# A cross-attention loop in another order: the last scores chunk, the context products and the running maxima

## The chip, the cores and the metric

The kernel runs on one core of a Trainium2 chip. A core has five engines with their own in-order instruction streams: TensorE (PE, with its weight loads listed apart as PEld), VectorE (DVE), ScalarE (ACT), GpSimd (POOL) and SyncE (SP), which issues the DMAs here. The metric is the device time of one execution in microseconds, as the median over repeated runs.

## The reference

The program is a two-layer perceiver step on 16 batches of 64 latent tokens (width 512) and 16 contexts of 1601 tokens (width 256). The change lies in the first of its six stages, the first cross attention with its output projection:

```python
def _L0_xattn_ref(q, k, v, Wq, bq, Wk, bk, Wv, bv, Wo, bo):
    HEADS = 16                       # D_MODEL = 512, D_K = 32
    qh = (q @ Wq + bq).reshape(B, LQ, HEADS, D_K).transpose(0, 2, 1, 3)
    kh = (k @ Wk + bk).reshape(B, LKV, HEADS, D_K).transpose(0, 2, 1, 3)
    vh = (v @ Wv + bv).reshape(B, LKV, HEADS, D_K).transpose(0, 2, 1, 3)
    scores = jnp.einsum('bhqd,bhkd->bhqk', qh, kh) * scale
    attn = jax.nn.softmax(scores, axis=-1)
    out = jnp.einsum('bhqk,bhkd->bhqd', attn, vh)
    concat = out.transpose(0, 2, 1, 3).reshape(B, LQ, D_MODEL)
    return concat @ Wo + bo

x = x + _L0_xattn_ref(_layernorm(x, axis=-1), ctx_512, ctx_512, ...)
```

Behind it come a state-space block, a top-k feed-forward, a second cross attention, a causal self attention and a quantized gated feed-forward. None of their code is touched.

## The kernel before

The first attention is a loop over 32 units `u` (and a 33rd pass that only finishes the last one). A unit is one batch and one half of the heads: eight heads, whose 8 x 64 = 512 query columns form the free dimension. Keys lie on the partitions, in 13 chunks (`KC`): twelve of 128 keys and a last one of 65. The loop is a software pipeline of two units: unit `u` gets its keys, values, scores and running maxima, while unit `u - 1` gets its softmax and its context.

What one pass issues:

- **K**: `k_proj` (L205), eight blocks of two matmuls, each drained by ACT (L215) out of a bank of `ps_mm`. Between the first of them stand `maxima(u - 1)` (L275: four transposes into the bank of `ps_mx`, then a DVE reduction, L281) and `shift(u - 1)` (L283: four more transposes, then seven DVE additions, L294).
- **V**: `v_proj` (L217), 13 chunks of two matmuls, each drained by a DVE addition of the bias (L226) out of a bank of `ps_mm`. `ps_mm` has two banks in rotation, for K, V and the output projection alike, so a block waits until the block two before it was drained.
- **Scores**: `scores(u, g)` (L235), groups of four chunks in the four banks of `ps_sc`, one buffer; the 13th chunk is a group of its own (`g` = 3). Two ACT copies (L252) bring a group to `st`, an SBUF tile of 13 x 512 per partition.
- **Running maxima**: `running_max(u, k)` (L263), DVE: L268 takes the chunks 0 to 3, L270 two more chunks at a time (128 x 1024), L273 the last one (65 x 512), and L486 folds the two halves together.
- **Exponentials and their sum**: `exps(u - 1, k)` (L297): ACT in place (L302), and POOL adds the chunks into `acc` (L307, four times L309, L311, L312).
- **Context**: `attend(u - 1, 0)` and `attend(u - 1, 1)` (L314), 52 small matmul calls each, and `sum_up` (L326), which multiplies `acc` by ones and so needs POOL's L312. `divide` (L333, DVE) ends the unit.
- **Beside it**: one 128 x 512 piece of a later stage's weights is quantized per pass: `piece_scale` (DVE L164 to L166, POOL L167), `piece_round` in the next pass (DVE L171, POOL L172), with a load and a store on SP's queue. `diagonal` (POOL L260, four copies) spreads the queries of the next unit. `load_ctx` (L187, SP) brings the context of the batch after next.

Passes 5, 9, 13 to 29 also hold an output projection `project` (L340: eight matmul instructions in the trace, drained by DVE L345), passes 18 to 21, 30 and 31 a layer norm and its transposes, and the first eight passes an addition on POOL (L423).

The order is written out by hand in the loop (L403 to L488): `pin` keeps each engine's instructions in the order of the text, and every engine works its own list from top to bottom. [...] two banks `ps_mm`, four `ps_sc`, one `ps_av`, one `ps_mx`.

Of the kernel before, what the change touches and what calls it, by code (L numbers as in the profile page):

```python
# [9 lines left out]
F32 = mybir.dt.float32  # L10
AF = mybir.ActivationFunctionType
ALU = mybir.AluOpType
# [3 lines left out]
P = 128  # L16
# [4 lines left out]
KC = (LK + P - 1) // P  # L21
# [21 lines left out]
def nkeys(c):  # L43
    return min(P, LK - c * P)
# [3 lines left out]
def perceiver_kernel(ctx: ExitStack, tc: tile.TileContext, x_d, ctxT_d, ctx_d, cols_d, rows_d,  # L48
# [3 lines left out]
    v, s, pe, gp = nc.vector, nc.scalar, nc.tensor, nc.gpsimd  # L52

    def pool(stack, name, bufs=1, side="left", **kw):
        return stack.enter_context(
            tc.tile_pool(name=name, bufs=bufs, side=side, reuse_waits="tile", **kw))
# [50 lines left out]
    st = const.tile([P, G, 6], F32, name="st", tag="st")  # L107
# [54 lines left out]
    def piece_scale(n, pin=free):  # L162
        w, sc, inv = raw[n]
        pin(v.tensor_reduce(sc, w, AX.X, ALU.max, apply_absolute_value=True))  # L164
        pin(v.tensor_scalar(sc, sc, 1.0 / 7.0, 1e-12, ALU.mult, ALU.max))
        pin(v.reciprocal(inv, sc))  # L166
        pin(gp.tensor_tensor(w, w, inv.unsqueeze(2).to_broadcast([P, 16, 32]), ALU.mult))  # L167
# [10 lines left out]
    with ExitStack() as st1:  # L178
# [18 lines left out]
        ps_mm = pool(st1, "ps_mm", bufs=2, space=PSUM)  # L197
        pin = tc.keep_in_program_order

        def pmm(out, lhsT, rhs, start=True, stop=True):  # L200
            pin(pe.matmul(out, lhsT=lhsT, rhs=rhs, start=start, stop=stop))  # L201

        kts, vts, sts, rms, nms, accs, avs = {}, {}, {}, {}, {}, {}, {}
# [24 lines left out]
        def flat(u):  # L228
            return sts[u]

        def by_head(t):

            return t.rearrange("p (r i j q) -> p r j i q", r=2, i=2, j=2)

        def scores(u, g):  # L235

            ks = range(4 * g, min(4 * g + 4, KC))
            m = nkeys(ks[-1])  # L240
            if g == 0:
                sts[u] = stp.tile([P, KC, 512], F32, name="st", tag="st")
            st = sts[u]
            sc = ps_sc.tile([P, 2, 4, 2 * P], F32, name="sc", tag="sc")
            for k in ks:
                for i in range(2):
                    for r in range(2):
                        rows_ = slice(64 * r, 64 * r + 64)
                        pmm(sc[:m, r, k - ks[0], i * P:(i + 1) * P],
                            kts[u, i][rows_, k * P:k * P + m], qds[u % 2][rows_, i, :])  # L250
            for r in range(2):
                pin(s.copy(st[:m, ks[0]:ks[-1] + 1, r * 256:(r + 1) * 256], sc[:m, r, 0:len(ks)]))  # L252

        def diagonal(u):

# [7 lines left out]
        def running_max(u, k):  # L263

            f = flat(u)
            if k == 2:
                rms[u] = mxp.tile([P, 2, 512], F32, name="rm", tag="rm")
                pin(v.tensor_tensor(rms[u], f[:, 0:2, :], f[:, 2:4, :], ALU.max))  # L268
            elif k + 1 < KC:
                pin(v.tensor_tensor(rms[u], rms[u], f[:, k:k + 2, :], ALU.max))  # L270
            else:
                m = nkeys(k)
                pin(v.tensor_tensor(rms[u][:m, 0], rms[u][:m, 0], f[:m, k, :], ALU.max))  # L273
# [23 lines left out]
        def exps(u, k):  # L297

            n = min(2, KC - k)
            m = nkeys(k + n - 1)  # L300
            f = flat(u)
            pin(s.activation(f[:m, k:k + n, :], f[:m, k:k + n, :], AF.Exp))  # L302
            if u == 2 * B - 1:
                return
            if k == 2:
                accs[u] = mxp.tile([P, 2, 512], F32, name="acc", tag="acc")
                pin(gp.tensor_tensor(accs[u], f[:, 0:2, :], f[:, 2:4, :], ALU.add))  # L307
            elif 2 < k and n == 2:
                pin(gp.tensor_tensor(accs[u], accs[u], f[:, k:k + 2, :], ALU.add))  # L309
            elif n == 1:  # L310
                pin(gp.tensor_tensor(accs[u][:, 0], accs[u][:, 0], accs[u][:, 1], ALU.add))  # L311
                pin(gp.tensor_tensor(accs[u][:m, 0], accs[u][:m, 0], f[:m, k, :], ALU.add))  # L312

        def attend(u, i):  # L314

            st = sts[u]
            if i == 0:
                avs[u] = ps_av.tile([P, 2, 2, LQ], F32, name="av", tag="av")
            for k in range(KC):
                n = nkeys(k)  # L320
                for j in range(4):
                    e = (4 * i + j) * 32
                    pmm(avs[u][32 * j:32 * j + 32, 0, i, :], vts[u, k][:n, e:e + 32],
                        by_head(st[:n, k, :])[:, j // 2, j % 2, i, :], k == 0, k == KC - 1)

        def sum_up(u, parts):  # L326

            for z, (t, n) in enumerate(parts):
                for j in range(4):
                    pmm(avs[u][32 * j:32 * j + 32, 1, :, :], ones[:n, 0:32],  # L330
                        by_head(t[:n, :])[:, j // 2, j % 2, :, :], z == 0, z == len(parts) - 1)
# [54 lines left out]
        for m in range(4):  # L386
            for r in range(2):
                j = 2 * (m % 2) + r
                nc.sync.dma_start(
                    out=wo0[32 * j:32 * j + 32, m // 2::2, :],  # L390
# [5 lines left out]
        qds = [mxp.tile([P, 2, P], F32, name="qd", tag=f"qd{i}") for i in range(2)]  # L396
# [4 lines left out]
        ps_mx = pool(st1, "ps_mx", space=PSUM)  # L401

        for u in range(U + 1):  # L403
            old, new = u >= 1, u < U
            k_at = iter(range(0, KC, 2))

            def next_exps(n):
                for _ in range(n if old else 0):
                    exps(u - 1, next(k_at))

            def next_k(i, z):
                if old and new:
                    k_proj(u, i, z)

            def next_v(*ks):
                for k in ks:
                    if old or k >= EARLY:
                        v_proj(u, k)

            if new:  # L420
                diagonal(u)
            if u < G:
                pin(gp.tensor_tensor(x[:, u, :], x[:, u, :], row(R_BO0), ALU.add))  # L423

            normed = [(g, ln_norm(g, pin)) for g in NORM0.get(u, ())]
            next_k(0, 0)
            if old:
                maxima(u - 1)
            next_k(0, 1)
            if old:  # L430
                shift(u - 1)
            next_k(0, 2)
            for g, xn in normed:
                ln_transpose(g, xn, ps_mm, pin)
            next_k(0, 3)
            for z in range(4):
                next_k(1, z)
                next_exps((1, 1, 0, 2)[z])
            if not new:

                next_exps(3)
                attend(u - 1, 0)
                attend(u - 1, 1)
                sum_up(u - 1, [(flat(u - 1)[:, k, :], nkeys(k)) for k in range(KC)])
                divide(u - 1)
                break
            if old and u <= NPREP:
                piece_round(u - 1, pin)
            if u < NPREP:
                piece_load(u, prep)  # L450
            next_v(0, 1)
            scores(u, 0)
            next_exps(2)
            next_v(2, 3)
            running_max(u, 2)
            next_v(4, 5)
            if u >= 2 and (u - 2) % 4 == 3:
                g = (u - 2) // 4
                project(g)
                ln_stats(g, pin)  # L460
                if g in (3, 6):
                    ln_scale(0 if g == 3 else 4, g + 1, pin)
            scores(u, 1)
            next_exps(1)
            next_v(6, 7)
            running_max(u, 4)
            next_v(8)
            running_max(u, 6)
            next_v(9)
            if u < NPREP:  # L470
                piece_scale(u, pin)
            if old:
                attend(u - 1, 0)
            scores(u, 2)
            next_v(10, 11)
            running_max(u, 8)
            next_v(12)
            running_max(u, 10)
            scores(u, 3)
            if u % 2 and u // 2 + 2 < B:  # L480
                load_ctx(u // 2 + 2)
            if old:
                attend(u - 1, 1)
                sum_up(u - 1, [(accs[u - 1][:, 0], P)])
            running_max(u, 12)
            pin(v.tensor_tensor(rms[u][:, 0], rms[u][:, 0], rms[u][:, 1], ALU.max))  # L486
            if old:
                divide(u - 1)  # L488
        project(G - 1)
# [172 lines left out]
    with ExitStack() as st3:  # L662
# [78 lines left out]
        for q in range(2):  # L741
# [29 lines left out]
            for k in range(4):  # L771
                g = 4 * q + k
# [16 lines left out]
    with ExitStack() as st4:  # L789
# [81 lines left out]
        ps_mm = pool(st4, "ps_mm4", bufs=3, space=PSUM)  # L871
# [89 lines left out]
    mx = const.tile([P, 5, 24], F32, name="mx", tag="mx")  # L961
# [125 lines left out]
    with ExitStack() as st6:  # L1087
# [121 lines left out]
        last = psc.tile([P, D], F32, name="po", tag="pm")  # L1209
# [90 lines left out]
```

## Time and profile before

| what | us |
|---|---|
| median of 3 runs | 2069.85 (2067.97 to 2070.45) |
| the profiled execution | 2068.01 |
| its span, first to last instruction | 2066.3 |
| passes 1 to 31 of the loop, 75.70 to 1174.20 in the trace | 1098.5 |
| PE busy in that stretch | 1083.0 |
| DVE / POOL / ACT busy in that stretch | 801.9 / 717.7 / 543.9 |
| a pass with nothing extra (890.07 to 924.19) | 34.12 |
| a pass with a projection (924.19 to 962.58) | 38.39 |
| a pass with a layer norm (676.86 to 711.99) | 35.13 |

The granted TensorE clock is 0.987 over the span and 1.00 within the loop. Times in the trace count from the first instruction. A timeline line gives the start, the length, the engine, the source line and the names of the tiles; a number in brackets is the idle time of the engine ahead of it and what ended it. Lengths include a wait inside the instruction, so the same instruction can have two lengths; PE's ends are modelled, so blocks of matmuls are compared by their starts. In the trace one pass repeats the last to within some hundredths of a microsecond.

### The profile page before, as it was taken

The numbers are of one execution on the slowest core, as the hardware profiler recorded it, in microseconds if no ns is written. First come the engines' busy times: TensorE is split into PE (matmuls) and PEld (weight loads), VectorE is DVE, ScalarE is ACT, GpSimd is POOL, SyncE is SP. The second block draws the span as 40 slices with busy tenths as digits, with TensorE's granted clock in tenths as the row PEclk, the third lists the DMA queues.
The fourth block names the chain that finished last, engine by engine and source line by source line (L and its number), as shares of the span: only waits on it lengthen the run. The fifth ranks groups of instructions, "written<-read, shape, count | busy, mean of one in ns | idle before, by whom it ended". The sixth has DMA issues, their size and how long they took to land. (4 is left out here: it accounts for less than half of the span.)

```text
span 2066.3 us, 38999 instructions
## 1 busy us (share of the span) xinstructions
PE 1970.2 (95%) x17197; PEld 1230.0 (60%) x17197; DVE 1192.8 (58%) x1710; ACT 805.3 (39%) x1112; POOL 793.9 (38%) x494
## 2 busy tenths in 40 slices
PE   8899999999999999999999898899998999999779
PEld 4677677677777676776777654444454455444334
DVE  2587777677776767786776744712113334429751
ACT  2445354545455454545454543211101123317700
POOL 0377667576667575675766421300003000000100
PEclk9999999999999999999999899999999999999889
DMA  5011101110110111011100120510227971200001
GB/s 207 27 49 53 44 12 54 43 36 30 54 44 22 44 53 44 16 50 43 46 20 17 33 103 22 186 61 21 94 98 272 339 292 62 72 0 11 20 0 41
DMA packets 61755, 141.13 MB, mean 68 GB/s; under 512 B 4449, under 2 KB 31601, under 8 KB 60433
## 3 DMA queue, kind: packets, MB, share of 16 engines
q1 hardware_dynamic: 61584, 138.63, 19.0%
q8 instruction: 135, 2.21, 0.5%
q14 instruction: 36, 0.29, 0.0%
HBM read 127.02 MB, written 11.60 MB: 67 GB/s over the span
## 5 line engine op out<-in xcount | busy, mean ns | idle before, releaser
L201 PE MATMUL ps<-wkv,ctxT 128*128 128x256 f32 (+1 forms) x1664 | 396.5, 387 | 2.0
L201 PE MATMUL ps<-ctxT,wkv 128*128 128x400 f32 (+1 forms) x1024 | 368.2, 506 | 10.9 <-DMA ctxT<-in_ctxT_dram 8.6
L252 ACT COPY st<-sc 128x1024 f32<-128x1024 f32 (+1 forms) x256 | 205.6, 854 | 353.7 <-PE sc L201 353.6
L201 PEld LDWEIGHTS ps<-wkv,ctxT 128*128 128x128 f32 (+1 forms) x1664 | 296.5, 185 | 76.3 <-ACT kt L215 13.8
L226 DVE TENSOR_TENSOR vt<-ps,rows 128x256 f32<-128x256 f32 (+1 forms) x416 | 170.3, 416 | 244.9 <-PE ps L201 244.8
L309 POOL TENSOR_TENSOR acc<-acc,st 128x1024 f32<-128x1024 f32 x124 | 292.4, 2358 | 8.3 <-ACT st L302 1.5
L201 PEld LDWEIGHTS ps<-ctxT,wkv 128*128 128x128 f32 x1024 | 187.4, 191 | 141.6 <-issue 12.7
L294 DVE TENSOR_TENSOR st<-st,nb 128x1024 f32<-128x1024 f32 (+1 forms) x224 | 238.9, 1138 | 24.7 <-PE nb L288 24.7
L215 ACT ACTIVATE kt<-ps,cols 128x400 f32<-128x400 f32 (+1 forms) x256 | 152.4, 595 | 243.0 <-PE ps L201 243.0
L270 DVE TENSOR_TENSOR rm<-rm,st 128x1024 f32<-128x1024 f32 x128 | 224.7, 1755 | 0.0
L201 PE MATMUL sc<-qd,kt 64*128 64x128 f32 (+1 forms) x3328 | 218.3, 279 | 2.1 <-ACT st L252 2.1
L302 ACT ACTIVATE st<-st 128x1024 f32<-128x1024 f32 (+1 forms) x224 | 216.0, 994 | 7.1 <-DVE st L294 6.7
L201 PEld LDWEIGHTS sc<-qd,kt 64*128 64x128 f32 (+1 forms) x3328 | 192.2, 183 | 41.6 <-issue 34.2
L307 POOL TENSOR_TENSOR acc<-st 128x1024 f32<-128x1024 f32 x31 | 84.5, 2727 | 302.4 <-ACT st L302 168.1
L260 POOL COPY qd<-xnT 32x128 f32<-32x128 f32 x128 | 107.0, 836 | 38.8 <-DVE xnT L380 33.8
L201 PE MATMUL av<-st,vt 128*32 128x64 f32 x6656 | 110.0, 223 | 4.8 <-ACT st L302 4.8
L59 PE MATMUL ps<-xnT,w 128*128 128x512 f32 x256 | 112.2, 594 | 0.0
L201 PEld LDWEIGHTS av<-st,vt 128*32 128x32 f32 x6656 | 98.4, 112 | 22.1 <-issue 15.6
L59 PE MATMUL ps<-w,hT 128*128 128x512 f32 x256 | 110.2, 592 | 0.0
L1184 POOL TENSOR_TENSOR gate<-up,gate 128x1024 f32<-128x1024 f32 x4 | 9.5, 2384 | 258.6 <-ACT up L1183 258.6
L859 POOL TENSOR_TENSOR xw<-x,wb 128x512 f32<-128x512 f32 x8 | 9.9, 1268 | 210.3 <-ACT wb L852 210.3
L59 PE MATMUL po<-wdT,gate 128*128 128x512 f32 x192 | 85.4, 608 | 3.2 <-DVE gate L1206 3.2
(233 smaller groups left out, 2278.8 us busy)
## 6 DMA issues: line engine op xcount, KB each, us to landing
cT<-in_ctxT_dram SPq DMA_DIRECT2D x16, 1601.0 KB, 10.0
cN<-in_ctx_dram SPq DMA_DIRECT2D x16, 1536.0 KB, 9.6
ctxT<-in_ctxT_dram SPq DMA_DIRECT2D x15, 1601.0 KB, 7.8
grid<-w SPq DMA_DIRECT2D x36, 256.0 KB, 2.0
w<-grid SPq DMA_DIRECT2D x36, 256.0 KB, 2.6
w<-in_w_dram SPq DMA_DIRECT2D x2, 4096.0 KB
mk<-kept SPq DMA_DIRECT2D x16, 512.0 KB, 3.8
w<-in_wgate_dram SPq DMA_DIRECT2D x12, 256.0 KB, 2.6
```

The source lines that it names most:

```text
L59: pe.matmul(out, lhsT=lhsT, rhs=rhs, start=start, stop=stop)
L201: pin(pe.matmul(out, lhsT=lhsT, rhs=rhs, start=start, stop=stop))
L215: pin(s.activation(kts[u, i][:, o:o + n], ps[:, :n], AF.Identity, bias=col(C_BK0 + c)))
L226: pin(v.tensor_tensor(t[:n, :], ps[:n, :], row(R_BV0 + e, 256)[:n, :], ALU.add))
L252: pin(s.copy(st[:m, ks[0]:ks[-1] + 1, r * 256:(r + 1) * 256], sc[:m, r, 0:len(ks)]))
L260: pin(gp.tensor_copy(qds[u % 2][r, :, (j % 2) * LQ:(j % 2 + 1) * LQ], qo[r, c:c + 2, b * LQ:(b + 1) * LQ]))
L270: pin(v.tensor_tensor(rms[u], rms[u], f[:, k:k + 2, :], ALU.max))
L294: pin(v.tensor_tensor(f[:m, k:k + n, :], f[:m, k:k + n, :], nb[:m].unsqueeze(1).to_broadcast([m, n, 512]), ALU.add))
L302: pin(s.activation(f[:m, k:k + n, :], f[:m, k:k + n, :], AF.Exp))
L307: pin(gp.tensor_tensor(accs[u], f[:, 0:2, :], f[:, 2:4, :], ALU.add))
L309: pin(gp.tensor_tensor(accs[u], accs[u], f[:, k:k + 2, :], ALU.add))
L859: gp.tensor_tensor(xw, x[:, g, :], wb, ALU.mult)
```

## The change

`scores(u, 2)` now also computes the 13th chunk. Its two results go to two extra PSUM tiles, one in the bank of `ps_mx` and one in a bank of `ps_mm`, which so joins the rotation as one more block; two more ACT copies follow the two of the group. `scores(u, 3)` is gone. In the loop:

- V's chunks 4 and 5 come ahead of `running_max(u, 2)`; chunks 8 and 9 come ahead of `running_max(u, 4)` and `(u, 6)`.
- `scores(u, 2)` stands ahead of the context, and `attend(u - 1, 0)`, `attend(u - 1, 1)` and `sum_up` follow it in one run.
- The maxima of the chunks 8 to 11 come ahead of V's chunks 10 and 11, and V's chunk 12 comes behind the last maxima (L273 and L486).
- `load_ctx` is issued behind V's chunk 12.

The number of matmuls, copies, additions and DMAs is the same.

```diff
-            ks = range(4 * g, min(4 * g + 4, KC))
-            m = nkeys(ks[-1])
+            ks = range(4 * g, 4 * g + 4)
+            last = KC - 1
...
-            for k in ks:
+
+            def one_chunk(out, k):
+                n = nkeys(k)
                 for i in range(2):
                     for r in range(2):
                         rows_ = slice(64 * r, 64 * r + 64)
-                        pmm(sc[:m, r, k - ks[0], i * P:(i + 1) * P],
-                            kts[u, i][rows_, k * P:k * P + m], qds[u % 2][rows_, i, :])
+                        pmm(out[r][:n, i * P:(i + 1) * P],
+                            kts[u, i][rows_, k * P:k * P + n], qds[u % 2][rows_, i, :])
+
+            for k in ks:
+                one_chunk([sc[:, r, k - ks[0], :] for r in range(2)], k)
+            if last == ks[-1] + 1:
+                tail = [ps_mx.tile([P, 2 * P], F32, name="scl", tag="mx"),
+                        ps_mm.tile([P, 2 * P], F32, name="scl", tag="mm")]
+                one_chunk(tail, last)
             for r in range(2):
-                pin(s.copy(st[:m, ks[0]:ks[-1] + 1, r * 256:(r + 1) * 256], sc[:m, r, 0:len(ks)]))
+                pin(s.copy(st[:, ks[0]:ks[-1] + 1, r * 256:(r + 1) * 256], sc[:, r]))
+            if last == ks[-1] + 1:
+                n = nkeys(last)
+                for r in range(2):
+                    pin(s.copy(st[:n, last, r * 256:(r + 1) * 256], tail[r][:n]))
...
-            next_v(2, 3)
+            next_v(2, 3, 4, 5)
             running_max(u, 2)
-            next_v(4, 5)
...
-            next_v(6, 7)
+            next_v(6, 7, 8, 9)
             running_max(u, 4)
-            next_v(8)
             running_max(u, 6)
-            next_v(9)
             if u < NPREP:
                 piece_scale(u, pin)
+            scores(u, 2)
             if old:
                 attend(u - 1, 0)
-            scores(u, 2)
+                attend(u - 1, 1)
+                sum_up(u - 1, [(accs[u - 1][:, 0], P)])
+            running_max(u, 8)
+            running_max(u, 10)
             next_v(10, 11)
-            running_max(u, 8)
+            running_max(u, 12)
+            pin(v.tensor_tensor(rms[u][:, 0], rms[u][:, 0], rms[u][:, 1], ALU.max))
             next_v(12)
-            running_max(u, 10)
-            scores(u, 3)
             if u % 2 and u // 2 + 2 < B:
                 load_ctx(u // 2 + 2)
-            if old:
-                attend(u - 1, 1)
-                sum_up(u - 1, [(accs[u - 1][:, 0], P)])
-            running_max(u, 12)
-            pin(v.tensor_tensor(rms[u][:, 0], rms[u][:, 0], rms[u][:, 1], ALU.max))
             if old:
                 divide(u - 1)
```

## The prediction

> **What bounds the kernel now.** First the page: its span and TensorE's share.
>
> ```profile
> span 2066.3 us, 38999 instructions
> PE 1970.2 (95%) x17197; PEld 1230.0 (60%) x17197; DVE 1192.8 (58%) x1710; ACT 805.3 (39%) x1112; POOL 793.9 (38%) x494
> ```
>
> Then the busy times by stretch (stretch, its length, PE, PEld, DVE, ACT, POOL, clock, DMA): a plain pass of the loop, one with a projection, one with a layer norm.
>
> ```profile
> 890.07:924.19 34.12, 34.01 (x416) 24.95 (x412) 26.07 (x34) 17.17 (x23) 23.59 (x14) 1.00 0.16 60
> 924.19:962.58 38.39, 37.50 (x424) 26.46 (x421) 25.66 (x38) 17.17 (x23) 21.11 (x16) 1.00 0.08 20
> 676.86:711.99 35.13, 34.64 (x420) 25.39 (x416) 25.47 (x35) 17.65 (x24) 22.90 (x12) 1.00 0.15 58
> ```
>
> TensorE sets the pass. Only what opens or closes a gap in its stream can move the time; DVE (26 of 34 us) and POOL (24) matter where TensorE waits for them. The gaps are read from the timeline, engine by engine, over the end of one plain pass (its K began at 856.07):
>
> ```profile
> 880.99 1.66 PE L201 MATMUL av<-st,vt 128*32 128x64 f32 x104
> ...
> 884.56 3.18 PE L201 MATMUL ps<-wkv,ctxT 128*128 128x256 f32 x12
> ...
> 890.07 1.61 PE L201 MATMUL ps<-ctxT,wkv 128*128 128x401 f32 x4
> ...
> 886.67 0.62 PEld L201 LDWEIGHTS ps<-wkv,ctxT 128*65 128x65 f32 x4 [0.51 <-DVE vt L226]
> ...
> 879.71 2.96 DVE L270 TENSOR_TENSOR rm<-rm,st 128x1024 f32<-128x1024 f32 x1
> ...
> 882.92 1.95 DVE L270 TENSOR_TENSOR rm<-rm,st 128x1024 f32<-128x1024 f32 x1
> ...
> 886.93 1.61 DVE L270 TENSOR_TENSOR rm<-rm,st 128x1024 f32<-128x1024 f32 x1
> ...
> 888.80 1.21 DVE L270 TENSOR_TENSOR rm<-rm,st 128x1024 f32<-128x1024 f32 x1
> ...
> 876.79 4.80 POOL L309 TENSOR_TENSOR acc<-acc,st 128x1024 f32<-128x1024 f32 x2
> ...
> 881.66 2.13 POOL L311 TENSOR_TENSOR acc<-acc 128x512 f32<-128x512 f32 x1
> 883.87 2.14 POOL L312 TENSOR_TENSOR acc<-acc,st 65x512 f32<-65x512 f32 x1
> 886.41 1.05 POOL L167 TENSOR_TENSOR w<-w,winv 128x512 f32<-128x512 f32 x1 [0.40 <-DVE winv L166]
> ```
>
> TensorE loses 0.3 us here at V's chunk 12, which waits for a bias addition (12 V matmuls take 3.18 us, 2.86 in the projection pass). The four equal maxima take 2.96, 1.95, 1.61 and 1.21: the last is alone, the others wait in line with POOL. The first ends (882.67) 1.08 after the last L309 (881.59), the second (884.87) 1.08 after L311 (883.79), the third (888.54) 1.08 after L167 (887.46); L311 and L312, alone 1.3 or less, end 1.1 after the maximum before them. [...]
>
> **The rule and the rows.** [...] a waiting POOL gets in between two dependent maxima. Pass 0 shows it:
>
> ```profile
> 77.50 0.69 DVE L273 TENSOR_TENSOR rm<-rm,st 65x512 f32<-65x512 f32 x1
> 77.64 1.68 POOL L423 TENSOR_TENSOR x<-x,rows 128x512 f32<-128x512 f32 x1
> 78.23 1.64 DVE L486 TENSOR_TENSOR rm<-rm 128x512 f32<-128x512 f32 x1
> ```
>
> L486 comes 0.04 after L273, is 0.69 long alone, and takes 1.64: POOL slipped in. I take turns throughout. Costs from these rows: maximum 1.08 behind POOL, 1.22 alone; L311 1.12 and L312 1.14 behind DVE; L167 1.05, or 0.90 behind DVE (L172, of its shape, ends 0.90 after a maximum).
>
> **The change, plain pass, TensorE.** From the first context block (880.99) to the next K (890.07) is 9.08 now. New order, no waits: group 2 with chunk 12, 1.99 + 4 pairs at 0.11 = 2.43; context twice, 1.48 each (888.26 to 889.74); sum 0.33; V10 to V12 2.79: total 8.51. Fewer switches between blocks of different shape make the 0.57. The K block ahead of the transposes then lacks its first 0.1 and a 0.05 wait, the transposes 0.05: -0.21. Without a wait, -0.78 a pass.
>
> **DVE and POOL decide whether there is one.** V9's addition ends at 881.51 (0.11 after its block, plus 0.42) and the first maximum comes up at 881.44, while L309 holds the way. Its end moves from 881.59 to 881.66: the L268 maximum, now behind V5's addition, comes at 875.81, level with L309, and delays it; I let DVE win, as L171 at 867.33 did against L307 of 867.14 (2.82 for 2.36). Then in turn: maximum to 882.74, L311 to 883.86, maximum to 884.94, L312 to 886.08. L165 is held to L312's end (885.84 with 0.21 did so now), L166 ends at 886.41. The maximum of chunks 8, 9 starts at 886.33, ahead of L167 (886.48): ends 887.55. L167 to 888.45, the maximum of 10, 11 to 889.53. Only then V10's addition, to 889.87. With the extra score tile in the rotation, V12 has V10's bank, so it starts at 889.93, not at the 888.56 of the unhindered order: **a new wait of 1.37**. V12 takes 0.93, and K starts at 890.86, 0.79 later than now; less 0.21, **+0.58 a pass**.
>
> Hidden: the sum's wait for L312 (886.08 against 886.37; late by up to 1.3, it would only use up V12's wait). ACT copies of group 2 end at 885.0, before the maxima want them, of chunk 12 at 885.6, before V11 wants that bank at 887.6. The transposes wait for L486, 891.54, and come up at 892.2; the second K block wants V12's addition, 891.9, at 892.7; the shift wants L281, 893.7, at 894.0: cover of 0.3 to 0.8, the next to be late. POOL's instructions keep their order, with no DMA among them. The context load goes out about 1 us later in the pass, nothing but the next pass's piece stands behind it on SP, its data is wanted two passes on, and it takes 7.8 us: 0.
>
> **Projection pass.** Now the projection waits for V5's addition, which stands behind L268:
>
> ```profile
> 944.55 0.70 PE L201 MATMUL ps<-wo,xnT 128*128 128x512 f32 x1 [0.89 <-DVE vt L226]
> ...
> 952.54 1.22 DVE L270 TENSOR_TENSOR rm<-rm,st 128x1024 f32<-128x1024 f32 x1
> ```
>
> The V block ahead of it takes 4.61 (939.94 to 944.55), against 3.65 without the wait: **-0.96**, since the addition comes first. POOL has L311 and L312 behind it before V9 is done (the maximum of 952.54 has its 1.22), so DVE is not held: L166 ends at 956.87 on the new clock of this pass, both maxima and L167 at 960.15, V10's addition at 960.49, V12 starts at 960.55 where 960.44 would be free. K at about 961.4 instead of 962.58; beyond the 0.96 that is -0.2, and -0.1 at the transposes: **-1.25**. Pass 21 loses only 0.6 at that wait now: -0.85.
>
> **Layer-norm pass.** Nothing waits at V12 now (2.79), and the turns fall as in the plain pass: V block to 703.24, V10's addition to 712.15, V12 1.4 late, K at 713.1 instead of 711.99; less 0.15: **+1.0**.
>
> **Sum.** 19 plain passes (1 to 4, 6 to 8, 10 to 12, 14 to 16, 22 to 24, 26 to 28) at +0.58: +11.0. Passes 18, 19, 20, 30 at +1.0: +4.0. Projections: 6 at -1.25 and one at -0.85: -8.3. The ends: pass 0 has no context to cover V12, but its transposes wait for L486 already (2.60): +1; pass 31 has no piece, so its maxima end earlier: -0.3; pass 6 loses its wait behind L423: -0.5. Together **+6.9 us**. The profiled execution is 2068.01 (2066.3 and 1.7 around it), 1.84 under the median and within the runs; I add to the median: 2069.85 + 6.9 = **2076.8**. About 0.2% (4.1 us) is what runs of this kernel can tell from no change: below 2065.7 is faster, above 2074.0 slower.
>
> **Rivals.**
>
> *The V12 wait doesn't come, since POOL doesn't get between dependent maxima.* Then DVE is through with both pairs sooner: second maximum of a pair at 883.9, and 888.8 for the last; V12 starts at 889.2, plain pass -0.16, layer-norm pass -0.3, projections as before: -3 - 1.2 - 8.3, **2057**, faster. For it: L486 at 890.83 keeps its 0.69 while a short L260 waits. Against it: L486 behind L423, above, an addition like L311. It decides if the maximum of 10, 11 ends under 888.5 or so on the clock of the plain pass. Chance 0.13.
>
> *No turns at all, or the bank is free anyway.* The waits vanish: 19 x -0.78, 4 x -0.5, -8.3: -25, **2045**. Every maximum row speaks against it, and the rotation of two banks is in the text. Chance 0.06.
>
> *POOL wins the tie at L268.* Then L268 ends at 879.2, V6's addition with it at 879.6, V8 waits 0.4 for the bank, and the later turns slip with it by another 0.2 to 0.7: plain pass +1.2 or more, 19 x 1.2 + 4 - 8.3 = +19, **2089**. A tie of 0.01 us; a POOL that begins 0.47 ahead wins for certain (the 2.96 row), one 0.19 ahead loses. Chance 0.17.
>
> *The parts cancel*: half the wait, or a larger gain at the projections. 2066 to 2074, chance 0.10.
>
> Mine has the rest, 0.54; its own range, from +-0.25 in a plain pass and +-0.3 in the others, is 2070 to 2083, a few hundredths of it under 2074. So faster 0.20, same 0.13, slower 0.67. From 2056 to 2091 leaves out the no-turns case and the tail beyond a lost tie.
>
> **What would show it.** In a plain pass of the profile after: V12's weight load waits 1.0 to 1.6 us for a bias addition, and its 12 V matmuls take 4.1, not 3.2; the gap before the transposes and before the projection is gone; the maximum of chunks 8, 9 takes 1.2 and that of 10, 11 near 1.9, right behind L167; the pass is 34.7 long, one with a projection 37.1, one with a layer norm 36.1. The steps are wrong if V12 waits under 0.5, if the sum waits for L312, if V8 waits for V6's addition, or if the transposes wait for L486 or the shift for L281, which would say that DVE is later than my turns make it.

## The result, and the profile after

The kernel after takes **2087.77 us** in the median against 2069.85 before: the ratio is 1.0093, with a 95% interval of 1.0078 to 1.0108, so it is 17.9 us slower. The profiled execution's span grew by 18.3 us, from 2066.3 to 2084.6. From the page of the kernel after, the span, the busy times and two groups (busy time and mean length, then the idle time ahead of them and what ended it):

```profile
span 2084.6 us, 38998 instructions
...
PE 1961.6 (94%) x17197; PEld 1238.9 (59%) x17197; DVE 1201.0 (58%) x1710; ACT 801.2 (38%) x1112; POOL 782.0 (38%) x494
...
L201 PE MATMUL ps<-wkv,ctxT 128*128 128x256 f32 (+1 forms) x1664 | 398.8, 388 | 15.4 <-DVE vt L226 14.0
...
L201 PEld LDWEIGHTS av<-st,vt 128*32 128x32 f32 x6656 | 99.6, 112 | 34.8 <-issue 28.5
```

The same two groups in the kernel before:

```profile
L201 PE MATMUL ps<-wkv,ctxT 128*128 128x256 f32 (+1 forms) x1664 | 396.5, 387 | 2.0
...
L201 PEld LDWEIGHTS av<-st,vt 128*32 128x32 f32 x6656 | 98.4, 112 | 22.1 <-issue 15.6 <-ACT st L302 6.4
```

TensorE is busy for 8.6 us less, which fits the forecast of fewer changes between blocks (an estimate, 0.57 us a plain pass), and yet the span is longer: it waits more. V's matmuls idled 2.0 us before and 15.4 now, 14.0 of it behind bias additions. The context's weight loads idled 22.1 us before, 15.6 of it under "issue"; it is 34.8 and 28.5 now. "Issue" is a wait for nothing that the profile shows.

Busy times by stretch in the kernel after (the same columns as before): three plain passes, one with a projection, one with a layer norm.

```profile
835.12:869.92 34.80, 33.59 (x413) 25.04 (x413) 25.46 (x35) 17.05 (x23) 22.70 (x13) 1.00 0.18 64
1011.80:1046.41 34.61, 33.48 (x413) 25.25 (x412) 24.84 (x35) 17.06 (x23) 22.77 (x14) 1.00 0.05 17
1046.41:1081.84 35.43, 33.69 (x413) 25.24 (x413) 25.27 (x35) 17.06 (x23) 22.58 (x13) 1.00 0.19 63
939.43:977.01 37.58, 37.13 (x421) 26.75 (x420) 25.57 (x38) 17.05 (x23) 21.00 (x13) 1.00 0.05 15
687.23:723.67 36.44, 34.56 (x417) 25.38 (x416) 27.71 (x36) 17.53 (x24) 22.74 (x15) 1.00 0.17 61
```

Before, the plain passes took 34.1 to 34.3, but for the first (35.0). Now there are kinds. The first, pass 22, is the forecast one. Its end in the timeline (start, length):

```profile
869.01 0.62 PEld L201 LDWEIGHTS ps<-wkv,ctxT 128*65 128x65 f32 x4 [1.61 <-DVE vt L226]
...
860.56 3.54 DVE L283 TENSOR_TENSOR rm<-rm,st 128x1024 f32<-128x1024 f32 x2
...
865.48 3.14 DVE L283 TENSOR_TENSOR rm<-rm,st 128x1024 f32<-128x1024 f32 x2
868.54 0.74 DVE L226 TENSOR_TENSOR vt<-ps,rows 128x256 f32<-128x256 f32 x2
...
865.64 1.90 POOL L167 TENSOR_TENSOR w<-w,winv 128x512 f32<-128x512 f32 x1 [0.40 <-DVE winv L166]
```

V12's weights wait for the additions of V10 and V11, which stand behind two pairs of maxima (L283, the former L270). A pair takes 3.54 and 3.14 us instead of twice 1.2, because POOL's instruction gets in between (L167 takes 1.90, not 1.05). By the starts of its matmuls V12 is 1.37 us late.

The other two plain passes, 27 and 28, have no wait at V12. They have a gap that nothing in the forecast explains, inside the context run. TensorE alone, first pass 27, then 28:

```profile
1039.03 3.10 PE L201 MATMUL av<-st,vt 128*32 128x64 f32 x202
1043.26 0.26 PE L201 MATMUL av<-st,vt 65*32 65x64 f32 x3 [1.13 <-issue]
...
1073.86 2.65 PE L201 MATMUL av<-st,vt 128*32 128x64 f32 x173
1078.25 0.69 PE L201 MATMUL av<-st,vt 128*32 128x64 f32 x34 [1.74 <-issue]
```

In pass 27 it stops after about 203 of 208 matmuls, for 1.35 us from start to start, in pass 28 after about 173, for 1.95. The matmuls behind the gap wait for no semaphore, and POOL's L325 (the former L312), which the sum needs, had ended at 1041.72 and 1076.57. The DMA view of the stretch around the first gap, 1040.85 to 1041.9, holds one packet:

```profile
DMA packets 1, 0.02 MB, mean 16 GB/s; under 512 B 0, under 2 KB 0, under 8 KB 0
## 3 DMA queue, kind: packets, MB, share of 16 engines
q8 instruction: 1, 0.02, 5.5%
```

It is a packet of 16,384 bytes on a queue that the profile calls "instruction", from 1040.90 to 1041.83; all 135 packets of that queue (q8) in the trace have this size, and from here on such a packet is called a page. The stretches on either side, 1039 to 1040.85 and 1041.9 to 1043.3, have no packet at all. TensorE goes on at 1043.26, 1.43 us after the page's end. There are 23 such gaps in the passes 1 to 31, 25.8 us in sum, and in all of them the last page had ended 1.25 to 1.57 us before TensorE went on. From one pass to the next the gap comes 30 matmuls earlier in the run (203, then 173).

### The profile page after: what moved, and what is told of

The parts are those of the page before. It is cut to its first block, busy times and chain, and to the rows that moved or that the text cites. A ratio compares the mean times of both kernels' runs of the same rounds, so it can differ in the third digit from the quotient of the medians.

```text
span 2084.6 us, 38998 instructions
## 1 busy us (share of the span) xinstructions
PE 1961.6 (94%) x17197; PEld 1238.9 (59%) x17197; DVE 1201.0 (58%) x1710; ACT 801.2 (38%) x1112; POOL 782.0 (38%) x494
## 5 line engine op out<-in xcount | busy, mean ns | idle before, releaser
L201 PE MATMUL ps<-wkv,ctxT 128*128 128x256 f32 (+1 forms) x1664 | 398.8, 388 | 15.4 <-DVE vt L226 14.0
L226 DVE TENSOR_TENSOR vt<-ps,rows 128x256 f32<-128x256 f32 (+1 forms) x416 | 174.5, 422 | 268.7 <-PE ps L201 267.7
L322 POOL TENSOR_TENSOR acc<-acc,st 128x1024 f32<-128x1024 f32 x124 | 323.6, 2610 | 8.3 <-ACT st L315 1.5
L261 ACT COPY st<-sc 128x1024 f32<-128x1024 f32 x192 | 185.1, 1016 | 249.4 <-PE sc L201 249.3
L283 DVE TENSOR_TENSOR rm<-rm,st 128x1024 f32<-128x1024 f32 x128 | 209.1, 1633 | 2.6
L201 PEld LDWEIGHTS sc<-qd,kt 64*128 64x128 f32 x3072 | 178.9, 188 | 36.8 <-issue 32.2
L201 PE MATMUL sc<-qd,kt 64*128 64x128 f32 x3072 | 197.3, 278 | 2.1 <-ACT st L261 2.1
L201 PEld LDWEIGHTS av<-st,vt 128*32 128x32 f32 x6656 | 99.6, 112 | 34.8 <-issue 28.5
L167 POOL TENSOR_TENSOR w<-w,winv 128x512 f32<-128x512 f32 x36 | 65.4, 1818 | 105.0 <-DVE winv L166 94.3
```

What stands on the lines that cost most here:

```text
L226: pin(v.tensor_tensor(t[:n, :], ps[:n, :], row(R_BV0 + e, 256)[:n, :], ALU.add))
L261: pin(s.copy(st[:, ks[0]:ks[-1] + 1, r * 256:(r + 1) * 256], sc[:, r]))
```

## Experiments

Two theories. TURNS is the prediction as it stands: DVE and POOL take turns (in the trace of before a maximum of 1.21 us took up to 2.96 behind an addition of POOL), V12 is late, and the gap is the same lateness seen elsewhere. SUPPLY adds that TensorE's instructions come in such pages (in the trace after, 255 instructions a page between the gaps of the passes 27 and 28), and that 208 small matmuls with 208 weight loads in a row use a page up faster than the next comes. Each run is compared with the kernel before on the same chip (medians there: 2071.64 for the first four, 2070.49 for the next four, 2072.64 for the last).

**V's chunks 4 and 5 first, alone.** On the kernel before:

```diff
-            next_v(2, 3)
+            next_v(2, 3, 4, 5)
             running_max(u, 2)
-            next_v(4, 5)
```

> The kernel before, with V's chunks 4 and 5 ahead of the first maximum and nothing else. The prediction's term: the projection no longer waits, 0.96 us in six passes and 0.6 in one, and DVE wins the near tie at L268 in the plain passes: 2062 to 2066 us. Rival: POOL wins the tie, V8 waits 0.4 us and later turns slip: 2068 to 2078 us.

2065.73 us, ratio 0.997 (0.9957 to 0.9982). The six projection passes lost 1.17 each, as the term of the prediction (0.96 and 0.1 to 0.2 at the next transposes) has it. The near tie at L268 fell both ways: in 5 of the 19 plain passes (4, 8, 10, 12, 28) V8 waits 0.47 us, which here costs little (34.30 instead of 34.20).

**The context split by the scores.** On the kernel after:

```diff
-            scores(u, 2)
             if old:
                 attend(u - 1, 0)
+            scores(u, 2)
+            if old:
                 attend(u - 1, 1)
```

> Two theories for the 18 us. TURNS (the prediction as it stands): DVE and POOL take turns, V12 waits for V10's addition, and the gap that the profile after shows inside the context run is only the same lateness seen at another place. SUPPLY: TensorE's instruction stream arrives in pages of 16 KiB, and a run of 208 small context matmuls with their weight loads uses one up faster than the next comes; the gap of 1.2 to 1.9 us in the run is that, and it comes on top wherever it is longer than V12's wait. Here the scores of the third group stand between the two context halves, all else as after. SUPPLY: no gap inside a context run, V12 waits 1.36 us in every plain pass, plain passes at 34.6 throughout, sum 19 x 0.5 + 4 x 1.0 - 7 x 1.1 + 1: 2074 to 2082 us. TURNS: 2085 to 2091, like the kernel after.

2095.64 us, ratio 1.0125 (1.0092 to 1.0159). The gaps are gone, all 23, as SUPPLY said, but the time went up, which neither theory said: V12 waits 1.65 us and most plain passes take 35.02 to 35.04. The scores now come 1.6 us later, and so do their copies. DVE and its first maximum (the timeline of DVE; the wait in brackets) show what follows:

```profile
1047.30 0.25 DVE L166 RECIPROCAL winv<-wsc 128x16 f32<-128x16 f32 x1
1047.75 3.27 DVE L283 TENSOR_TENSOR rm<-rm,st 128x1024 f32<-128x1024 f32 x2 [0.20 <-ACT st L261]
```

The maximum waits for the copy, which ends at 1047.72, and the pair takes 3.27 instead of 3.14. The experiment took one wait away and lengthened another, so its time says nothing on the size of the gaps.

**The piece's scale moved.** On the kernel after; L164 to L167 leave the place ahead of V10's addition:

```diff
             if old:
                 maxima(u - 1)
+                if u <= NPREP:
+                    piece_scale(u - 1, pin)
             next_k(0, 1)
...
-            if u < NPREP:
-                piece_scale(u, pin)
```

> The kernel after, with the piece's scale (L164 to L167) moved into the next pass between the maxima and the shift, where POOL is idle; this takes 1.1 us of DVE work and one turn of POOL out from ahead of V10's addition. TURNS: V12's wait falls from 1.36 to 0.2 to 0.5 us, a plain pass takes 33.6 to 33.9, in all 2052 to 2058 us. SUPPLY: V12's wait falls as well, but the gaps in the context run (26 us over all passes after) are now uncovered and stay: 2070 to 2080 us, with passes of 33.7 and of 34.6 to 35.4 side by side.

2075.2 us, ratio 1.0017 (1.0009 to 1.0026). V12's wait fell from 1.37 to 0.45 us where it stands, and without a gap a plain pass takes 33.9 (10, 14, 22, 26), 34.3 (6) or 34.53 (2). The passes with a gap take 34.4 to 35.4, and the gaps still sum to 23.4 us. V12's weight load in pass 26, then the context run in pass 27:

```profile
997.88 0.62 PEld L201 LDWEIGHTS ps<-wkv,ctxT 128*65 128x65 f32 x4 [0.68 <-DVE vt L226]
...
1026.04 3.10 PE L201 MATMUL av<-st,vt 128*32 128x64 f32 x202
1030.15 0.26 PE L201 MATMUL av<-st,vt 65*32 65x64 f32 x3 [1.02 <-issue]
```

The time lies in SUPPLY's range; TURNS alone had 2052 to 2058. The lateness of DVE and the gaps are two things: two thirds of the first are gone, nearly all of the second is left.

A caution holds for this trace and for those of two runs below ("Both" and "POOL's turn alone"): between 1580 and 1600 us, in a later stage, the granted clock was 0.83 (1.00 there before), and the time behind the loop is 4.7 to 7.1 us longer than before. Up to the end of the loop they are 3.1, 3.5 and 4.2 us behind the trace of before, in this order.

**Both.** The first split and the moved scale together, on the kernel after:

```diff
                 maxima(u - 1)
+                if u <= NPREP:
+                    piece_scale(u - 1, pin)
...
-            if u < NPREP:
-                piece_scale(u, pin)
-            scores(u, 2)
             if old:
                 attend(u - 1, 0)
+            scores(u, 2)
+            if old:
                 attend(u - 1, 1)
```

> Both edits of the two runs before together. SUPPLY and TURNS together: neither the gap in the context run nor most of V12's wait: 2050 to 2060 us, faster than the kernel before. If it stays above 2068, a third cause is at work.

2076.08 us, ratio 1.0022 (1.0014 to 1.0031), above the range: no gap, but V12 waits 0.87 us. The third cause is the late copy again, now with nothing ahead of it on DVE:

```profile
1030.58 2.48 DVE L283 TENSOR_TENSOR rm<-rm,st 128x1024 f32<-128x1024 f32 x2 [1.67 <-ACT st L261]
```

The first split was a bad one for that reason; the next leaves the scores where they are.

**The context split by V10 and V11.** On the kernel after; DVE's order stays, TensorE's changes:

```diff
                 attend(u - 1, 0)
-                attend(u - 1, 1)
-                sum_up(u - 1, [(accs[u - 1][:, 0], P)])
             running_max(u, 8)
             running_max(u, 10)
             next_v(10, 11)
+            if old:
+                attend(u - 1, 1)
+                sum_up(u - 1, [(accs[u - 1][:, 0], P)])
```

> The kernel after, with V's chunks 10 and 11 between the two context halves on TensorE; DVE's order and the third group's scores stay where they are, so unlike the first split this one delays no copy. SUPPLY: the context comes in two runs of 104 again, no gap in either, V12 waits 1.0 to 1.4 us for V10's addition in every plain pass (+0.5 us a pass), 2074 to 2082 us. TURNS: nothing but V12's wait decides, 2085 to 2091 us like the kernel after.

2078.48 us, ratio 1.0042 (1.0025 to 1.0058). No gap is left. 14 of the 19 plain passes take 34.60 to 34.62; four (8, 11, 23, 24) lose the tie at L281 and take 35.4; pass 1 takes 36.25. V12 waits:

```profile
1033.23 1.50 PEld L201 LDWEIGHTS av<-st,vt 128*32 128x32 f32 x104 [0.17 <-issue]
...
1036.75 1.50 PEld L201 LDWEIGHTS av<-st,vt 128*32 128x32 f32 x104 [0.33 <-issue]
...
1039.69 0.41 PEld L201 LDWEIGHTS ps<-wkv,ctxT 128*65 128x65 f32 x3 [1.33 <-DVE vt L226]
```

So this is the kernel after without the gaps, and it is +8.0 us against the kernel before on its chip; the forecast without them was +6.9. That these lie so close is in part luck: up to the end of the loop the trace is 9.7 us behind that of before, and the rest of the program is 2.1 us shorter.

**Pages shifted.** On the kernel after, 128 more TensorE instructions ahead of the loop:

```diff
+        more = ps_mx.tile([P, 64], F32, name="more", tag="mx")
+        for _ in range(32):
+            pmm(more, ident, ident[:, 0:64])
         for u in range(U + 1):
```

> The kernel after, with 32 small matmul calls (64 matmuls and 64 weight loads, 128 instructions, half a page) ahead of the loop, which nothing reads; some 4 us of extra work, nothing else changed. SUPPLY: the gaps in the context run move to other passes, since every page now ends 64 matmuls earlier in the program: passes 8, 12, 16, 20, 24 and 28, with gaps of 1.2 to 1.9 us after, have none, and passes 10, 14, 22 and 26, with none after, have 1.2 to 1.9. TURNS: the same passes have gaps as after, because no DVE or POOL instruction has moved.

The passes 8, 12, 16, 20, 24 and 28 have no gap; 10, 14, 22 and 26 have 1.53, 1.51, 1.72 and 1.12. Pass 28, where the kernel after stopped for 1.95, and pass 26, where it did not stop:

```profile
1084.84 3.12 PE L201 MATMUL av<-st,vt 128*32 128x64 f32 x208
...
1015.04 2.55 PE L201 MATMUL av<-st,vt 128*32 128x64 f32 x167
1018.49 0.78 PE L201 MATMUL av<-st,vt 128*32 128x64 f32 x41 [0.91 <-issue]
```

No DVE or POOL instruction was moved, so TURNS can't explain this. The single time is 2100.3 us. About 7 of the 12.5 us above the kernel after lie ahead of the loop's first transposes: the 64 added matmuls took 7.2 us (59.09 to 66.28), not the 4 expected. The projection passes, which had short gaps, now have 1.2 to 1.9 us.

**V10 and V11 between, and the piece moved.** On the kernel after:

```diff
                 maxima(u - 1)
+                if u <= NPREP:
+                    piece_scale(u - 1, pin)
...
-            if u < NPREP:
-                piece_scale(u, pin)
...
                 attend(u - 1, 0)
-                attend(u - 1, 1)
-                sum_up(u - 1, [(accs[u - 1][:, 0], P)])
             running_max(u, 8)
             running_max(u, 10)
             next_v(10, 11)
+            if old:
+                attend(u - 1, 1)
+                sum_up(u - 1, [(accs[u - 1][:, 0], P)])
```

> The same with the piece's scale moved into the next pass between the maxima and the shift. With SUPPLY and TURNS both right neither the gap nor most of V12's wait is left: V12 waits under 0.4 us, a plain pass takes 33.5 to 33.9, 2050 to 2060 us, faster than the kernel before. If a plain pass stays above 34.1, a third cause is at work.

**2047.37 us**, ratio 0.9902 (0.9883 to 0.9922): the fastest of all, 1% under the kernel before and below the range. From the tenth pass on a plain pass takes 33.57 (pass 28; the projection pass behind it 36.91):

```profile
1016.44:1050.01 33.57, 33.55 (x413) 25.16 (x412) 24.89 (x34) 17.05 (x23) 22.69 (x13) 1.00 0.19 66
1050.01:1086.92 36.91, 36.91 (x421) 26.68 (x420) 26.35 (x40) 20.03 (x26) 23.07 (x13) 1.00 0.05 16
```

or 34.03 in the four where V8 waits. With both waits that the change made out of the way, a plain pass is 0.55 us shorter than before. The forecast put the fewer changes between blocks at 0.57 and a pass without any wait at -0.78. How much of the 0.55 is due to those changes alone is not shown, since this kernel also splits the context again and has the piece moved.

**The order of before, with both good parts.** On the kernel before, V's chunks 4 and 5 first and the piece's scale moved:

```diff
                 maxima(u - 1)
+                if u <= NPREP:
+                    piece_scale(u - 1, pin)
...
-            next_v(2, 3)
+            next_v(2, 3, 4, 5)
             running_max(u, 2)
-            next_v(4, 5)
...
-            if u < NPREP:
-                piece_scale(u, pin)
```

> The kernel before with V's chunks 4 and 5 ahead of the first maximum and the piece's scale moved into the next pass, the rest of the loop as before (context halves apart, chunk 12 of the scores on its own). TURNS and SUPPLY agree: V12's wait of 0.3 us and the waits at K and at the transposes go (-0.4 to -0.5 us in a plain pass), the projections gain 1.2 us each, no gap in the context runs: 2050 to 2058 us.

2060.96 us, ratio 0.9961 (0.9948 to 0.9973), just above the range: plain passes of 33.78 from the seventh on, but 34.67 in 2, 3, 4 and 6 and 37.67 in 1, and layer-norm passes 0.2 to 0.5 longer than before, not traced further. The change's order with V10 and V11 between is 13.6 us faster than this one by the medians. By the traces 9.0 us of it have come by the end of the loop, 2.7 of these in pass 1, where the granted clock of this run was 0.79 between 75 and 82 us (1.00 in the other).

**POOL's turn alone.** On the kernel with V10 and V11 between; only L167 is moved on POOL, behind the next pass's query copies, and DVE keeps its work and order:

```diff
         pin(v.reciprocal(inv, sc))
-        pin(gp.tensor_tensor(w, w, inv.unsqueeze(2).to_broadcast([P, 16, 32]), ALU.mult))
...
             if new:
                 diagonal(u)
+            if old and u <= NPREP:
+                piece_times(u - 1, pin)
```

> The kernel with V's chunks 10 and 11 between the context halves (2078.5 us), with POOL's L167 alone moved behind the next pass's query copies; DVE keeps L164 to L166 where they are, so DVE has exactly the same work in the same order. TURNS: L167 no longer gets in between the maxima of chunks 8, 9 and 10, 11, the second of them takes 1.2 instead of 1.95 us, V10's addition and V12 come 0.75 us earlier, a plain pass takes 33.8 to 34.0 instead of 34.6, 2058 to 2065 us. If DVE's own work and not POOL's turn made V12 late, nothing changes: 2076 to 2081 us.

2073.38 us, ratio 1.0006 (0.9996 to 1.0017), above the range. The second pair of maxima takes 2.42 us instead of 3.14, with DVE's work unchanged: these 0.7 us were POOL's turn, as TURNS said. But much of it is lost again a few instructions on. DVE first, then POOL, then the transposes' weight load:

```profile
1031.22 2.42 DVE L288 TENSOR_TENSOR rm<-rm,st 128x1024 f32<-128x1024 f32 x2
...
1034.93 1.42 DVE L499 TENSOR_TENSOR rm<-rm 128x512 f32<-128x512 f32 x1
...
1034.21 1.60 POOL L172 TENSOR_TENSOR w<-w,winv 128x512 f32<-128x512 f32 x1
...
1036.41 0.42 PEld L297 LDWEIGHTS mt<-ident,rm 128*128 128x128 f32 x4 [0.60 <-DVE rm L499]
```

The moved multiplication (here L172) slips in between the last maximum and the fold (L499, 1.42 for 0.69), and the transposes wait for that; 12 plain passes take 34.4, six 34.0 to 34.2, the first 36.9. A turn that is moved is not a turn that is gone.

## Why the prediction was right, and where it fell short

The sign and the mechanism held: slower, because V12 waits. V12's wait was put at 1.37 us and is 1.37 in pass 22; POOL does get in between dependent maxima (the pair takes 3.14 us with L167 in between, 2.42 where only L167 is moved); the projection's 0.96 is gone in every projection pass (from the V block ahead of it to the projection 3.56 us in all seven; 4.60 to 4.62 before, 4.26 in pass 21). The size did not hold: the forecast move was 6.9 us and the measured one 17.9. The time lies inside 2056 to 2091 only because that range was drawn around the rivals; the range of the mechanism itself, 2070 to 2083, is missed. That the rival of a lost tie stood at 2089 is chance as well: POOL won that tie in two of the plain passes, not in all.

The sum, in us of the traces (against the trace of before; a pass is taken from its first transposes to the next pass's):

| term | predicted | after | after with V10, V11 between |
|---|---|---|---|
| 19 plain passes | +11.0 | +17.4 | +13.2 |
| passes 18, 19, 20, 30 | +4.0 | +5.3 | +4.7 |
| 7 projection passes | -8.3 | -6.2 | -9.1 |
| pass 0, to the first transposes | +1.0 | +1.0 | +1.8 |
| pass 31 | -0.3 | +0.9 | -0.9 |
| pass 6, a term of its own | -0.5 | in the plain passes | in the plain passes |
| together | +6.9 | +18.3 | +9.7 |

Pass 0 agrees by accident: between 75 and 82 us the granted clock of the kernel after was 0.55 (1.00 before), and from V12 to the transposes it took 4.4 us, against 2.3 in the next pass. By these two lengths the term would be about -1.2 at full clock, an estimate.

The step that failed is "context twice, 1.48 each", and with it the total of 8.51, in the 23 passes with a gap. The 1.48 was the length of one run of 104 matmuls between other blocks, and two of them on end were taken to be twice that. The two make 416 instructions in 2.94 us when nothing is missing (pass 22). Between the gaps of the passes 27 and 28 TensorE issued 383 matmuls and as many weight loads, and three pages came: 255 instructions a page. The whole trace agrees: 17197 matmuls, as many weight loads and 135 pages make 255 as well. At 416 instructions in 2.94 us a page lasts 1.8 us in such a run, an estimate from these counts. In pass 27 the next one came into use later than that: the matmul one page ahead of the gap, by this count, started at 1040.06; the page came from 1040.90 to 1041.83 and TensorE went on at 1043.26, 3.2 us after 1040.06. 3.2 less 1.8 is 1.4; the gap is 1.35. In the order of before the longest such run in the passes 1 to 31 has 104 matmuls and 104 weight loads, under one page, and there is no such gap in them.

The gaps sum to 25.8 us and cost 9 to 10 us net (+17.9 against +8.0 by the medians, +18.3 against +9.7 in the table), because where V12 would have waited 1.37 anyway, a gap of 1.3 costs nothing. That is why pass 27, with a gap, is as long as the forecast pass (34.61; 34.60 to 34.62 with V10 and V11 between and no gap): the cover of 1.3 us that the prediction named for the sum's wait for L312 was used up by something else.

Two smaller points. The tie at L268 (now L281) was called for DVE. Of the plain passes it went to POOL in 4 and 14. Pass 14, DVE, POOL and TensorE:

```profile
564.10 3.44 DVE L281 TENSOR_TENSOR rm<-st 128x1024 f32<-128x1024 f32 x1
...
564.10 5.66 POOL L322 TENSOR_TENSOR acc<-acc,st 128x1024 f32<-128x1024 f32 x2
...
567.93 1.59 PEld L201 LDWEIGHTS ps<-wkv,ctxT 128*128 128x128 f32 x8 [0.70 <-DVE vt L226]
```

L281 takes 3.44 and V8 is late, by 0.47 from start to start. The rival put such a pass at +1.2; with V10 and V11 between, where no gap disturbs, it is +1.27 (35.39 against 34.12), and four of 19 lose the tie. And the cover of 0.3 us at the shift was too thin in the kernel after: many passes lose 0.1 to 0.2 there, as in pass 22, which is 0.2 longer than 34.6. With V10 and V11 between, none does.

## What to carry to other kernels

A run of small instructions can have a price that none of its instructions shows, as the 23 gaps of 25.8 us here: count the instructions per microsecond of the densest stretch before putting two such stretches together, and look at the instruction queue's packets when an engine waits long for "issue". Where two engines take turns, as the maxima of DVE and the additions of POOL did here, lay their instructions out on one clock; lengths that include a wait give the turns away (1.21 us alone, 1.61 to 2.96 in turn), and here the new wait could be forecast to a few hundredths from them (1.37 forecast, 1.37 in pass 22). An addition that drains a PSUM bank belongs ahead of work that nobody waits for (V5's ahead of the first maximum: 1.17 us in each of six projection passes); if it must stand behind, take something else out from ahead of it, and check what takes the turn that comes free.

## What the runs showed of the hardware

TensorE went on 1.25 to 1.57 us after the end of the last page of 16,384 bytes in all 23 gaps of the kernel after, whose length (0.28 to 1.95 us) moves with the place of the page's end in the run. The profile puts these gaps under "issue". That they were a wait for instructions rests on this and on the run with pages shifted, where 128 more TensorE instructions ahead of the loop took the gap out of six passes and put 1.12 to 1.72 us into four others. The pauses of 0.17 and 0.33 us ahead of the context's weight loads, which stand under "issue" too, were none of these: there are 62, 15.6 us in sum, in the kernel before as in the one with V10 and V11 between, and neither has a gap. What sets the moment at which a page is asked for stays open: by the count of 255 instructions, the page started 0.8 us after the page ahead of it came into use in the passes 27 and 28, 1.3 us after in pass 8 (gap 1.89), and up to 0.6 us ahead of that in passes with a short gap (0.3 in pass 5); no run varied that alone. When DVE's L281 and POOL's L322 came up within 0.01 us of each other, either went first: L281 in pass 28 (1066.25 against 1066.24; it took 1.22 us), L322 in pass 14 (both at 564.10; L281 took 3.44). Where POOL came 0.28 to 0.37 us ahead of it (passes 1, 18 to 21, 30 and 31), POOL went first each time, and L281 took 3.08 to 3.16 us.
